# Norm squares of q in batch 1 get slots of hS, and the turning of x of batch 3 is cut in two

## The chip, the core and the metric

The kernel runs on one core of one Trainium2 chip. The metric is the device time of one execution in microseconds (us); the kernel before has a median of 606.14 us over three runs (606.14, 606.62 and 604.99). Five instruction streams run beside each other and meet only at semaphores: TensorE (PE; its weight loads are PEld), VectorE (DVE), ScalarE (ACT), GpSimd (POOL) and SyncE (SP). SP does no arithmetic here: it issues DMAs. ACT issues some DMAs too, and does so in the same stream as its arithmetic. Each stream is executed in the order in which the program wrote it.

## What is computed

Eight batches of x, each 1024 tokens by 256 channels, all float32. Cut to what matters:

```python
xn  = layernorm(x)                                   # no weights
q, k, v = split(xn @ qkv_w + qkv_b)                  # 16 heads of 16 channels
q, k = l2norm(q), l2norm(k)                          # per token and head
kv  = einsum('bhnd,bhne->bhde', k, v)                # linear attention, 16x16 per head
att = einsum('bhnd,bhde->bhne', q, kv) @ proj_w + proj_b
ffn = relu(xn @ W1 + b1) @ W2 + b2                   # 256 -> 1024 -> 256
out = x + att + ffn
```

## The kernel before

**Products by sums.** Nearly all matrix products are done with fewer block products than the plain way: the blocks of both operands are added and subtracted first, and the results are added up afterwards. Those of q and k, of xn^T kn and of the output are 2x2 schemes with seven products (`project_by_sums`, `mix_g_by_sums`, `second`); the hidden layer of batches 1 to 7 is a scheme with 26 products, the list `PRODUCTS`, played out by the list `STEPS` (`hidden`). PE has less to do for it, and DVE, ACT and above all POOL have the sums: POOL makes the forms of x (`FORMS`, L307: s1A, X1 to X10 and so on), those of the hidden layer, and those of xn and kn.

**Stages.** For each batch b the order on PE is: `hidden(b)` (W1 and relu), `project_by_sums(b + 1)` (q and k of the next batch), and `second(b)` (W2 and the projection of the attention, L1112), in the middle of which `mix_g_by_sums(b + 1)` makes g = xn^T kn of the next batch. v is never made: kv comes from g and the weights (`mix_kv`, L755), and `mix_m` (L774) folds it with proj_w into a matrix M that stands beside W2.

**Order by hand.** There is no scheduler: `tc.manual_schedule()` keeps the order of the source on each engine. What is not a matrix product is handed to `second` and `hidden` as callbacks that are played at fixed points. For `second` they are `early`, `mid`, `behind`, `late` and `later` (L1420 to L1460), and where they stand is what this change is about. In `second(b)` the order is: product a, copy u1, product c, `early()`, add u2, product a again, y, `mid()`, turn_back, `behind()`, products f and d, add u3, join(1,0), then six of the seven products of g (`next(of_g)`, L1283), `more_sums_of_x(b + 1, 0)` (X3 to X6 on POOL), `late()`, product e, join(1,1), the seventh product of g, `more_sums_of_x(b + 1, 1)` (X7 to X10 on POOL), `later()`, store of half the output, product e again, join(0,1). A join adds on DVE, transposes 32x32 blocks on DVE (`turn_back`) and adds to the output tile xq on POOL (L1147).

**The norm of q.** `norms_of_q(b)` (L608) squares q of a batch in four pieces of 128x512 on ACT (`squares_of`, L504), sums each piece by head on DVE (L505), inverts the 128x128 sums (`invert`: maximum on DVE L465, root on ACT L466, reciprocal on DVE L467) and scales q on POOL in two halves (`scale`, L624). The squares go to two small buffers that alternate, so the third square waits for the sum of the first; for batch 1 these are the tags `u1` and `y`, for the others the two buffers of `yt`. For batch 1 all this is in `later()` of `second(0)`, after X7 to X10; for later batches it is in `early()`. The scaled q is then turned (`turn_of_q`, four DVE transposes L386, each moved by four DMAs L394) during the next `hidden`, between its sums.

**The turning of x.** `turn_x(b)` does a quarter of the transposition of xn: one DVE transpose of 128x512 (L386) into the tile `turn`, then four DMAs of 64 KB (L394) that carry the squares to xnT. `turn_next()` (L1414) does four of them for batch b + 2 and then `shift` (ACT, L656), which adds one to half of xn. In `second(0)` it stands in `late()` with half of the DMAs on ACT, in `second(1)` in `behind()`, from `second(2)` on in `early()`; there all DMAs are SP's. In `second(1)` it turns batch 3, whose normalization stands just ahead (`mid()`: statistics L344 to L359 and eight ACT applications L368).

**What follows on the queues.** `late()` ends with `load(b + 3)`: two SP DMAs of 512 KB of x (L149). In `second(1)` this is x of batch 4, and `later()` takes its statistics on DVE (`stats_of(4)`: L344, L347, L356, L359) ahead of join(0,1) and of the sums of `hidden(2)` (L1004). SP's next issues are the output store (L1110), the weights of the hidden layer that are loaded anew for each batch (w_sb<-w1f, L898), the second store and the moves of the turned q.

**Slots.** `hS[b]` holds sums of the hidden layer and of q: three kinds by five slots of 128x512. In batch 0 the third kind is free after `first_hidden`; slots 0 to 3 of it hold s1, s4, t1 and t2 of the sums of xn and kn of batch 1 (`g_sums`, L700), and slot 4 (`FH`) held a sum of x. Slots 0, 2 and 3 (s1, t1 and t2) are read last by the first six products of g; s4 in slot 1 is read by the seventh.

Of the kernel before, what the change touches and what calls it, by code (L numbers as in the profile page):

```python
# [9 lines left out]
F32 = mybir.dt.float32  # L10
# [51 lines left out]
def kernel(  # L62
# [35 lines left out]
    P = 128  # L98
    B, N, C = x.shape
    H, D = 16, 16  # L100
    assert H * D == C
    INTER = w1.shape[1]
    NT = N // P
# [6 lines left out]
    R = P // S  # L110
# [7 lines left out]
    one = ctx.enter_context(tc.tile_pool(name="one", bufs=1))  # L118
    work = ctx.enter_context(tc.tile_pool(name="work", bufs=2))
    small = ctx.enter_context(tc.tile_pool(name="small", bufs=2))  # L120
# [19 lines left out]
    xs, xqs, xns, xnTs, xSs, hTs, qks, qTs, mixes, Ms, hSs = ({} for _ in range(11))  # L140
# [105 lines left out]
    HM, FH, HC = INTER // 2, FC // 2, C // 2  # L246
# [46 lines left out]
    def forms_of(b):  # L293

        f = {f"b{k + 1}{u + 1}": xnTs[b][:, k, u, :, :] for k in range(KC) for u in range(NP)}
        f |= {v: xS[:, i] for i, v in enumerate(("s1A", "s2A", "s4A", "s1B", "s2B", "s4B"))}
        f |= {v: as_tokens(half_of_w1t(1, i)) for i, v in enumerate(("dA", "s3B"))}
        f |= {"X1": f["b21"], "X2": f["b14"]}
        return f

    def more_forms_of(b):

        return {
            f"X{3 + i}": qks[b][:, 1, i, :].rearrange("p (c w) -> p c w", w=2) for i in range(8)
        }
# [10 lines left out]
    def make_forms(f, names):  # L316
        for v in names:
            p, op, q = FORMS[v]
            nc.gpsimd.tensor_tensor(f[v], f[p], f[q], ALU.add if op == "+" else ALU.subtract)
# [7 lines left out]
    def more_sums_of_x(b, part):  # L327

        names = [f"X{i}" for i in range(3 + 4 * part, 7 + 4 * part)]
        make_forms(forms_of(b) | more_forms_of(b), names)  # L330
# [45 lines left out]
    class Turn:  # L376
# [21 lines left out]
        def step(self, queues=(nc.sync,)):  # L398
            self.square()
            self.move(queues)  # L400
# [62 lines left out]
    def invert(ss):  # L463

        nc.vector.tensor_scalar_max(ss, ss, L2_EPS * L2_EPS)  # L465
        nc.scalar.activation(ss, ss, AF.Sqrt)  # L466
        nc.vector.reciprocal(ss, ss)  # L467
# [29 lines left out]
    def part_of_qk(b, u, m):  # L497

        return qks[b][:, m, 2 * u : 2 * u + 2, :]

    def squares_of(b, u, m, ss, tag="yt"):
        pool = work if tag == "yt" else one
        sq = pool.tile([P, 2, C], F32, tag=tag, name=f"sq_{b}_{u}_{m}")
        nc.scalar.activation(sq, part_of_qk(b, u, m), AF.Square)  # L504
        return lambda: nc.vector.tensor_reduce(  # L505
            ss[:, 2 * u : 2 * u + 2, :],
            sq.rearrange("p w (g d) -> p w g d", d=D), AX.X, ALU.add,
        )
# [85 lines left out]
    def bias_of_q(b, bias=None):  # L594
        if bias is None:
            bias = bias_in_bank(b)
        for u in (3, 0):
            q1 = part_of_qk(b, u, 0)
            nc.vector.tensor_tensor(
                q1, q1, bias.unsqueeze(1).to_broadcast([P, 2, C]), ALU.add  # L600
            )

    def bias_in_bank(b):
        bias = bank([P, C], f"dbias_{b}")
        nc.scalar.copy(bias, dbias)
        return bias

    def norms_of_q(b):  # L608
        ss = small.tile([P, NT, H], F32, tag="ssq", name=f"ssq_{b}", bufs=1)
        late = []  # L610
        for u in range(NP):
            late.append(squares_of(b, u, 0, ss, ("u1", "y")[u % 2] if b == 1 else "yt"))
            if len(late) == 2:
                late.pop(0)()
        late.pop(0)()
        invert(ss)
        for h in range(2):
            norms_of[b, h, 0] = ss[:, ts(h, HT), :]
            scale(nc.gpsimd, b, h, 0)

    def scale(eng, b, h, s):

        part = qks[b][:, s, ts(h, HT), :].rearrange("p t (g d) -> p t g d", d=D)
        eng.tensor_tensor(  # L624
            part, part,
            norms_of[b, h, s].unsqueeze(3).to_broadcast([P, HT, H, D]), ALU.mult,
        )
# [8 lines left out]
    def turn_q(b):  # L636
        turn_of_q(b).step()
# [15 lines left out]
    def shift(b):  # L653

        part = xns[b][:, :, 0:P]
        nc.scalar.activation(part, part, AF.Identity, bias=ones)  # L656
# [443 lines left out]
    def product(dst, lhs, rhs, start, stop):  # L1100

        for n, (l, r) in enumerate(zip(lhs, rhs)):
            nc.tensor.matmul(  # L1103
                dst, l, r, start=start and n == 0, stop=stop and n == len(lhs) - 1,
                skip_group_check=True,
            )
# [5 lines left out]
    def second(b, early=None, mid=None, behind=None, late=None, later=None):  # L1112
# [16 lines left out]
        def tmp(name):  # L1129
            pool = work if name in ("u2", "yt") else one  # L1130
            return pool.tile([P, HP, P, 2], F32, tag=name, name=f"{name}_o_{b}")
# [5 lines left out]
        def turn_back(n, m, y):  # L1137

            yt = tmp("yt").rearrange("p a b c -> p (a b c)").rearrange(
                "p (u w r c) -> p u w r c", w=2, r=R, c=S  # L1140
            )
            nc.vector.transpose(  # L1142
                yt.rearrange("p u w r c -> p u r w c"),
                y.rearrange("p u (s r) w -> p u r w s", r=R),
            )
            xh = xq[:, n, :, :, ts(m, S)].rearrange("p r t c -> p t r c")
            nc.gpsimd.tensor_tensor(xh, xh, yt.rearrange("p u w r c -> p (u w) r c"), ALU.add)  # L1147

        def join(n, m, bank_, u):
            y = tmp("y")  # L1150
            nc.vector.scalar_tensor_tensor(y, bank_, ob[:, 2, m : m + 1], u, ALU.add, ALU.add)  # L1151
            turn_back(n, m, y)
# [107 lines left out]
        def po(s):  # L1260
            return bank([P, HP, P, 2], f"po{s}_{b}")
# [3 lines left out]
        u1 = tmp("u1")  # L1265
# [5 lines left out]
        y = tmp("y")  # L1271
# [4 lines left out]
        f = po("f")  # L1276
# [10 lines left out]
        product(e, t1, s1, True, False)  # L1287
        join(1, 1, e, u3)
        next(of_g)
        more_sums_of_x(b + 1, 1)  # L1290
        later()
        store(b, 1)
        product(e, b22, s4, False, True)
        join(0, 1, e, u2)


    warm = bank([P, HT, P], "warm")
# [23 lines left out]
    i, mv, rstd = stats.pop((0, 0))  # L1321
# [58 lines left out]
    for b in range(B):  # L1380
        if b == 0:
            first_hidden()
            nc.sync.dma_start(out=w1_sb[:, 0, HM:INTER], in_=w1[0:P, HM:INTER])
        else:
            hidden(b)
        if b == B - 1:
            for _ in second(b):
                pass
            break

        def load_first_w1():
            load_w1(0, 4)
            load_w1(4, 1)

        if b == 0:

            def last_turn():
                turn_q(0)
                sums_of_q(0, "1")
                for i in range(FH):  # L1400
                    sums_of_h(0, i, "2")
                sums_of_q(0, "2")

            of_w1 = forms_of_w1()
            project_by_sums(1, [lambda: turn_q(0), last_turn])
            next(of_w1)
        else:
            load_first_w1()
            load_squares(b)
            if b > 1 and b + 2 < B:  # L1410
                norm_apply(b + 2, range(NT))
            project_by_sums(b + 1)

        def turn_next():  # L1414
            if b + 2 < B:
                for _ in range(R):
                    turn_x(b + 2, (nc.sync, nc.scalar) if b == 0 else (nc.sync,))
                shift(b + 2)

        def early():  # L1420
            g_sums(b + 1, 1)
            g_sums(b + 1, 2)
            for i in (1, 2, 0, 3):
                sums_of_h(b, i, "3")
            sums_of_q(b, "3")
            if b == 0:
                next(of_w1)
                stats_of(2)
                return
            bias_of_q(b + 1)  # L1430
            norms_of_q(b + 1)
            if b > 1:
                turn_next()

        def mid():
            if b == 0:
                norm_apply(2, range(NT))
                next(of_w1)
                load_first_w1()
            elif b == 1:  # L1440
                stats_of(3)
                norm_apply(3, range(NT))

        def behind():
            if b == 1:
                turn_next()

        def late():
            if b == 0:
                bias = bias_in_bank(1)  # L1450
                turn_next()
                bias_of_q(1, bias)
            if b + 3 < B:
                load(b + 3)

        def later():
            if b == 0:
                norms_of_q(1)
            else:
                stats_of(b + 3)  # L1460

        second(b, early, mid, behind, late, later)


# [29 lines left out]
```

## Time and profile before

| what | us |
|---|---|
| median of three runs | 606.14 (604.99 to 606.62) |
| the profiled execution, its own time | 604.75 |
| its span, first to last instruction | 603.0 |
| PE busy | 596.5 |
| POOL busy | 481.0 |
| DVE busy | 435.4 |
| ACT busy | 247.4 |
| granted TensorE clock | 1.000 throughout |

The profile is one execution on the chip: its start and end outside the span make 1.75 us. A line of a timeline gives the start and the length in us, the engine, the source line, the operation, the tile that is written and those that are read, the shape, and how many instructions were merged (x4); in brackets at its end stands how long the engine was idle before it and what released it. "SPq" and "ACTq" are DMA issues. PE instructions are pipelined, so that the length of a group overlaps with the next one's; the distance of starts tells the pace: 0.86 us for a product of the hidden layer or of q and k, 0.89 us for one of g, 4.29 us for one of `second`. The stages that are spoken of lie at: `second(0)` from 67 to 104 us, `hidden(1)` from 104 to 130, `second(1)` from 142 to 179, `hidden(2)` from 179 to 204.

### The profile page before, as it was taken

Reading aid. Unit: us, or ns where it says so; the run is one execution under the profiler, and the core shown is the slowest. Engines: PE = TensorE matmul, PEld = TensorE weight load, DVE = VectorE, ACT = ScalarE, POOL = GpSimd, SP = SyncE. Lnnn points to the kernel's source line nnn. Section 1 sums busy time; section 2 is a strip of 40 time slices with the busy share of each in tenths; the row PEclk is TensorE's granted clock in tenths of the full one; section 3 lists DMA queues with packets and bytes.
Section 4 is the critical chain, followed back from the end, with each engine's and each line's share of the span. In section 5 each row is a group of like instructions: output and inputs, shape, how many; then the busy total and the mean of one; then the engine's idle time right before and its main releaser. Section 6 shows DMA issues by size and latency. Waiting matters only on the chain.

```text
span 603.0 us, 7997 instructions
## 1 busy us (share of the span) xinstructions
PE 596.5 (99%) x2385; PEld 413.2 (69%) x2385; DVE 435.4 (72%) x803; ACT 247.4 (41%) x525; POOL 481.0 (80%) x453
## 2 busy tenths in 40 slices
PE   9999999999999999999999999999999999999997
PEld 5466656786568865688566894678846787468746
DVE  7987976878758785577856878388873669537773
ACT  4654332473405851158311673126730373203810
POOL 2859999988976889769897698976989679983470
PEclk9999999999999999999999999999999999999999
DMA  8545367784056733377134780356702667006704
GB/s 289 87 101 140 82 211 206 183 210 55 10 158 170 194 48 70 108 202 179 19 71 139 197 172 6 99 137 178 158 22 49 144 144 148 2 0 164 185 11 95
DMA packets 164810, 73.02 MB, mean 121 GB/s; under 512 B 147488, under 2 KB 152736, under 8 KB 163872
## 3 DMA queue, kind: packets, MB, share of 16 engines
q1 hardware_dynamic: 154432, 67.31, 46.6%
q10 hardware_dynamic: 10336, 5.21, 3.1%
q8 instruction: 19, 0.31, 0.2%
q14 instruction: 23, 0.19, 0.1%
HBM read 44.44 MB, written 11.80 MB: 93 GB/s over the span
## 4 chain that ended last, share of the span: by engine, by line
PE 86%; DVE 6%; POOL 3%; DMA 2%; ACT 1%; issue 1%; ACTq 0%; DVEq 0%; POOLq 0%
PE ph L985 23%; PE poe L1103 9%; PE poa L1103 9%; PE pod L1103 5%; PE poc L1103 5%; PE pof L1103 4%; PE pqe L530 3%; PE pqa L530 3%; PE pqd L530 3%; PE gpd L728 2%; PE gpe L728 2%; PE gpa L728 2%; PE pqc L530 2%; POOL qk L624 2%; PE tok L1213 2%; PE pq L428 1%
## 5 line engine op out<-in xcount | busy, mean ns | idle before, releaser
L1012 ACT ACTIVATE hT<-hT,b_sb 128x256 f32<-128x256 f32 x224 | 95.7, 497 | 56.1 <-DVE hT L1004 56.1
L1004 DVE TENSOR_TENSOR hT<-ph,hT 128x512 f32<-128x512 f32 x84 | 56.0, 687 | 25.1 <-ACT hT L999 21.6
L1004 DVE TENSOR_TENSOR hT<-hT,ph 128x512 f32<-128x512 f32 x77 | 51.8, 679 | 11.1 <-PE ph L985 7.0
L1103 PE MATMUL poa<-hT,w_sb 128*128 128x512 f32 x120 | 56.2, 593 | 0.0
L504 ACT ACTIVATE sq<-qk 128x512 f32<-128x512 f32 x56 | 34.2, 627 | 49.9 <-DVE qk L536 39.8
L1147 POOL TENSOR_TENSOR xq<-xq,yt_o 128x512 f32<-128x512 f32 x29 | 36.5, 1272 | 22.1 <-DVE yt_o L1142 22.1
L985 PE MATMUL ph<-xnT,w_sb 128*128 128x256 f32 x224 | 52.9, 379 | 0.0
L985 PE MATMUL ph<-qk,w_sb 128*128 128x256 f32 x196 | 48.1, 379 | 0.3 <-DMA w_sb<-w1f 0.3
L239 POOL TENSOR_TENSOR hS<-hT 128x512 f32<-128x512 f32 x30 | 38.3, 1276 | 11.5 <-DVE hT L1004 11.5
L985 PEld LDWEIGHTS ph<-xnT,w_sb 128*128 128x128 f32 x224 | 41.9, 190 | 5.5
L985 PEld LDWEIGHTS ph<-qk,w_sb 128*128 128x128 f32 x196 | 37.2, 190 | 5.7 <-POOL Mt L234 0.7
L999 ACT COPY hT<-ph 128x512 f32<-128x512 f32 x49 | 28.1, 574 | 30.4 <-PE ph L985 30.3
L240 POOL TENSOR_TENSOR hS<-hS,hT 128x512 f32<-128x512 f32 x30 | 38.3, 1277 | 2.4
L1103 PEld LDWEIGHTS poa<-hT,w_sb 128*128 128x128 f32 x120 | 22.7, 190 | 25.4 <-issue 22.7
L242 POOL TENSOR_TENSOR hT<-hT 128x512 f32<-128x512 f32 x30 | 38.5, 1310 | 0.0
L1142 DVE STREAM_TRANSPOSE yt_o<-y_o 128x512 f32<-128x512 f32 x29 | 32.2, 1112 | 8.3 <-ACT y_o L1272 6.1
L244 POOL TENSOR_TENSOR hS<-hT,hS 128x512 f32<-128x512 f32 x30 | 37.7, 1290 | 0.0
L985 PE MATMUL ph<-xS,w_sb 128*128 128x256 f32 x140 | 35.1, 381 | 0.2
L624 POOL TENSOR_TENSOR qk<-qk,ssk 128x1024 f32<-128x1024 f32 x14 | 26.8, 1936 | 9.3 <-DVE ssk L467 9.3
L1151 DVE SCALAR_TENSOR_TENSOR y_o<-poe,ob,u_o 128x512 f32<-128x512 f32 x14 | 10.4, 741 | 31.1 <-PE poe L1103 31.1
L1103 PE MATMUL poe<-hS,w_sb 128*128 128x512 f32 x64 | 30.4, 600 | 0.3
L1103 PE MATMUL poc<-hS,w2t 128*128 128x512 f32 x64 | 29.9, 592 | 0.0
(249 smaller groups left out, 1422.4 us busy)
## 6 DMA issues: line engine op xcount, KB each, us to landing
w_sb<-w1f SPq DMA_DIRECT2D x49, 256.0 KB, 3.5
qT<-turn_q SPq DMA_DIRECT2D x128, 64.0 KB, 3.0
x<-in_L_attn_x_dram SPq DMA_DIRECT2D x15, 512.0 KB, 4.6
xq<-in_L_attn_x_dram SPq DMA_DIRECT2D x60, 128.0 KB, 5.0
out_dram<-xq SPq DMA_DIRECT2D x58, 128.0 KB, 2.9
w_sb<-w1f SPq DMA_DIRECT2D x7, 1024.0 KB, 4.9
xnT<-turn_x SPq DMA_DIRECT2D x104, 64.0 KB, 2.1
w1t<-w1f SPq DMA_DIRECT2D x14, 256.0 KB, 5.3
```

What stands on the lines that cost most here:

```text
L239: eng.tensor_tensor(s1, a21, a22, ALU.add)
L240: eng.tensor_tensor(s2, s1, a11, ALU.subtract)
L242: eng.tensor_tensor(a21, a11, a21, ALU.subtract)
L244: eng.tensor_tensor(s4, a12, s2, ALU.subtract)
L530: nc.tensor.matmul(dst[:, w, :], f[pairs[g][2][i]][:, :, w], pairs[g][3][i], start=start and w == 0, stop=stop, skip_group_check=True,)
L624: eng.tensor_tensor(part, part, norms_of[b, h, s].unsqueeze(3).to_broadcast([P, HT, H, D]), ALU.mult,)
L728: nc.tensor.matmul(dst, l[:, t, :], r[:, t, :], start=start and t == 0, stop=stop and t == HT - 1, skip_group_check=True,)
L985: nc.tensor.matmul(banks[chain][:, t], w[:, t, :], f[v], start=start and t == 0, stop=n == last[chain], skip_group_check=True,)
L1004: nc.vector.tensor_tensor(block(v), operand(p), operand(q), ALU.add if op == "+" else ALU.subtract)
L1012: nc.scalar.activation(part, part, AF.Relu, bias=b1_sb[:, fc : fc + 1])
L1103: nc.tensor.matmul(dst, l, r, start=start and n == 0, stop=stop and n == len(lhs) - 1, skip_group_check=True,)
L1147: nc.gpsimd.tensor_tensor(xh, xh, yt.rearrange("p u w r c -> p (u w) r c"), ALU.add)
```

## The change

It has two parts.

1. **q of batch 1.** Its four squares go to slots 0, 2, 3 and 4 of the third kind of hS of batch 0, one slot each, instead of alternating between two buffers. The squares stand in `late()` of `second(0)` and their sums, the inversion and the scaling in `later()`, through a generator. For b = 0 alone `more_sums_of_x(1, 1)`, the forms X7 to X10, moves from ahead of `later()` to the end of `second`, behind join(0,1).
2. **x of batch 3.** `turn_next` in `behind()` of `second(1)` does two of the four quarters and no shift; the other two and the shift move to `late()`, behind six of the seven products of g and ahead of `load(4)`.

On PE the order of instructions is the same in both kernels. On ACT the four squares stay behind the DMA issues and the shift, and the shift of batch 3 moves behind the two copies of g. On POOL the two scalings of q of batch 1 and the last xq addition stand ahead of the four instructions of X7 to X10. On DVE two of the four transposes of x of batch 3 move behind four additions of g. On SP the order of DMAs is the same.

```diff
-    def squares_of(b, u, m, ss, tag="yt"):
-        pool = work if tag == "yt" else one
-        sq = pool.tile([P, 2, C], F32, tag=tag, name=f"sq_{b}_{u}_{m}")
+    def squares_of(b, u, m, ss, sq=None):
+        if sq is None:
+            sq = work.tile([P, 2, C], F32, tag="yt", name=f"sq_{b}_{u}_{m}")
         nc.scalar.activation(sq, part_of_qk(b, u, m), AF.Square)
...
+    def norms_of_second_q():
+
+        ss = small.tile([P, NT, H], F32, tag="ssq", name="ssq_1", bufs=1)
+        late = [
+            squares_of(
+                1, u, 0, ss,
+                hSs[0][:, 2, i].rearrange("p u c w -> p (u c w)").rearrange("p (w c) -> p w c", w=2),
+            )
+            for u, i in enumerate((0, 2, 3, FH))
+        ]
+        yield
+        for step in late:
+            step()
+        invert_and_scale_q(1, ss)
+        yield
...
         next(of_g)
-        more_sums_of_x(b + 1, 1)
+        if b > 0:
+            more_sums_of_x(b + 1, 1)
         later()
         store(b, 1)
         product(e, b22, s4, False, True)
         join(0, 1, e, u2)
+        if b == 0:
+            more_sums_of_x(b + 1, 1)
...
-        def turn_next():
+        of_q = []
+
+        def turn_next(n=R, shifted=True):
             if b + 2 < B:
-                for _ in range(R):
+                for _ in range(n):
                     turn_x(b + 2, (nc.sync, nc.scalar) if b == 0 else (nc.sync,))
-                shift(b + 2)
+                if shifted:
+                    shift(b + 2)
...
         def behind():
             if b == 1:
-                turn_next()
+                turn_next(2, False)

         def late():
             if b == 0:
                 bias = bias_in_bank(1)
                 turn_next()
                 bias_of_q(1, bias)
+                of_q.append(norms_of_second_q())
+                next(of_q[0])
+            elif b == 1:
+                turn_next(2)
             if b + 3 < B:
                 load(b + 3)

         def later():
             if b == 0:
-                norms_of_q(1)
+                next(of_q[0])
             else:
                 stats_of(b + 3)
```

`invert_and_scale_q` is the last part of `norms_of_q`, unchanged and given a name.

More of the change, by code (lines that the diff above doesn't have):

```diff
@@ L611, in norms_of_q @@
         for u in range(NP):
-            late.append(squares_of(b, u, 0, ss, ("u1", "y")[u % 2] if b == 1 else "yt"))
+            late.append(squares_of(b, u, 0, ss))
             if len(late) == 2:
@@ L615, in norms_of_q, with invert_and_scale_q @@
         late.pop(0)()
+        invert_and_scale_q(b, ss)
+    def norms_of_second_q():
[12 more added lines that the diff above has]
+        yield
+    def invert_and_scale_q(b, ss):
         invert(ss)
```

## The prediction

> **What bounds the kernel.** I read the page's first part, then PE's waits over the whole span, then the chain of work by time, then the timelines of all engines from 90 to 205 us. First the page:
>
> ```profile
> span 603.0 us, 7997 instructions
> PE 596.5 (99%) x2385; PEld 413.2 (69%) x2385; DVE 435.4 (72%) x803; ACT 247.4 (41%) x525; POOL 481.0 (80%) x453
> ```
>
> and the list of what PE waited for (total us, times, longest):
>
> ```profile
> PE warm L1298 <- DVE ones L216: 1.1, 1, 1.1
> PE ph L985 <- DVE hT L1004: 0.7, 2, 0.4
> PE gpd L728 <- DVE u_g L734: 0.6, 1, 0.6
> PE ph L985 <- DMA w_sb<-w1f: 0.3, 1, 0.3
> ```
>
> TensorE is the bound. Its waits come to 2.7 us in all, and 1.6 of them lie where the change is made; no other edit of cover can win anything. The restart after a wait costs more than the wait, so I price stages by starts. `hidden(3)` runs on PE from 252.93 to 277.14: 24.21 us, no wait. `hidden(2)` takes 179.20 to 204.27: 25.07, so 0.86 is lost. `hidden(1)` takes 103.77 to 129.70: 25.93, so 1.72 is lost. In `second(1)`, from the fifth product of g (166.81) to the next product (169.44) it is 2.63 us; in `second(2)` the same steps take 241.39 to 243.17, 1.78; so 0.85 is lost. The change can touch 3.4 us, or 0.57%, and no more.
>
> The waits on PE's timeline:
>
> ```profile
> 112.98 1.10 PE L985 MATMUL ph<-xnT,w1t 128*128 128x256 f32 x4 [0.38 <-DVE hT L1004]
> ...
> 119.25 1.97 PE L985 MATMUL ph<-qk,w_sb 128*128 128x256 f32 x8 [0.30 <-DMA w_sb<-w1f]
> ...
> 168.47 1.13 PE L728 MATMUL gpd<-gt,x 128*128 128x128 f32 x8 [0.60 <-DVE u_g L734]
> ...
> 188.29 1.10 PE L985 MATMUL ph<-xnT,w1t 128*128 128x256 f32 x4 [0.27 <-DVE hT L1004]
> ```
>
> Four stalls are to be seen: two in `hidden(1)`, one in g of batch 2, one in `hidden(2)`.
>
> **Part 1, q of batch 1.** What leads to the scaling, from the timelines of ACT, DVE and POOL:
>
> ```profile
> 101.05 1.15 ACT L656 ACTIVATE x<-x,ones 128x1024 f32<-128x1024 f32 x1 [7.19 <-DMA xnT<-turn_x]
> 102.10 1.14 ACT L504 ACTIVATE sq<-qk 128x512 f32<-128x512 f32 x2
> 103.47 1.22 ACT L504 ACTIVATE sq<-qk 128x512 f32<-128x512 f32 x2 [0.23 <-DVE ssq L505]
> ...
> 102.75 2.67 DVE L505 TENSOR_REDUCE ssq<-sq 128x32 f32<-128x512 f32 x4 [2.11 <-ACT sq L504]
> ...
> 107.08 3.83 POOL L624 TENSOR_TENSOR qk<-qk,ssq 128x1024 f32<-128x1024 f32 x2 [0.81 <-DVE ssq L467]
> ```
>
> POOL waited 0.81 us for the reciprocal, so X7 to X10, done by 106.28, are not what holds the scaling. What holds it are the squares, and these start when ACT has issued its DMAs and done the shift (102.1); the new order leaves both ahead of them. All that goes is the third square's wait of 0.23. DVE's sums are nearly back to back already: starts at 102.75, 103.35 and 104.14, then 0.60 more. With four free slots they go at 0.60 throughout, and the fourth ends 3 x 0.60 + 0.69 behind 102.75, at 105.24 instead of 105.43. The scaling comes **0.19 us** earlier.
>
> Two things follow it. DVE's turn_q at 110.95 waits for POOL, and PE's wait at 112.98 is for an addition behind it: 0.19 off. The last xq addition on POOL, the store and two weight loads behind it on SP (112.18, 114.89) move by 0.19 too, and the wait at 119.25 is for those weights. The two stalls lie one behind the other, so the end of the stage moves by 0.19, not by twice that.
>
> What it costs: X7 to X10 (2.91 us on POOL, 103.37 to 106.28) now come after the xq addition, at about 112.0 to 114.9. X7 is PE's product 19, at about 123.6: covered by 8 us. POOL's next work (g_sums, s3B, s1A, M's sums, s2A and so on) comes 2.9 late and meets POOL's own waits: 1.43 us at 123.03, 0.57 at 126.63, 1.55 at 147.36. Its first forms of batch 2 that PE reads, s1B and s2B, would be done at about 125, and PE asks for them at 130.56. So I cost it at nothing; if this cover were gone, 2.9 less those waits.
>
> Two additions of hT by hT (114.89, taking 1.08, and 116.52, taking 0.64) run beside POOL, and two at 190.22 while POOL waits take 1.28 together. So POOL's work costs the first about 0.44 today. Now POOL's 1.28 us instructions of g_sums stand there. If one addition waits for such a whole instruction, 0.85 more than now, products 13 and 14 (117.82, 119.25) go late, and past the cover of 0.3 some 0.5 is left. If neither waits, 0.44 is won on DVE, but the weights still end the wait. I take -0.19 for part 1; ends -0.3 and +0.5. The nearest row, turn_q to scaling, is the reason.
>
> [...]
>
> **Part 2, x of batch 3.** DVE and SP in `second(1)` and `hidden(2)`:
>
> ```profile
> 162.68 2.49 DVE L386 STREAM_TRANSPOSE turn_x<-x 128x512 f32<-128x512 f32 x4 [3.07 <-ACT x L368]
> ...
> 169.64 0.29 DVE L734 TENSOR_TENSOR gT<-gpd,u_g 128x128 f32<-128x128 f32 x1 [0.99 <-PE gpd L728]
> 173.93 0.75 DVE L1151 SCALAR_TENSOR_TENSOR y_o<-poe,ob,u_o 128x512 f32<-128x512 f32 x1 [4.00 <-PE poe L1103]
> ...
> 177.68 1.41 DVE L344 BATCH_NORM_STATS2 st<-x 128x6 f32<-128x256 f32 x4 [1.61 <-DMA x<-in_L_attn_x_dram]
> ...
> 163.42 10.50 SPq L394 DMA_DIRECT2D xnT<-turn_x  x16
> 174.09 0.96 SPq L149 DMA_DIRECT2D x<-in_L_attn_x_dram  x2
> ```
>
> The gain: four transposes hold DVE from 162.68 to 165.10, 0.605 each. Two fewer bring what follows 1.21 earlier. The addition of u_g at 168.03 comes at 166.97, when PE's fourth product of g is out (166.81 and 0.16 for its tail), and ends by 167.3; PE is ready for the sixth at 167.70. The stall goes: **0.85 us**. The other transposes fall into DVE's idle 4.00 us ahead of 173.93, the shift into ACT's idle 13 us: both free.
>
> The loss is on SP. Its 16 DMAs take 10.50 us, 0.656 each, and x of batch 4 is issued right behind them. Now the ninth waits for the third transpose: the gT addition at 169.64 - 0.85 = 168.79, the transpose 0.21 later (as in `second(0)`, 94.21 to 94.42), the DMA 0.74 after that (162.68 to 163.42): 169.74. Eight more take 5.25, to 174.99; the load follows 0.17 later (173.92 to 174.09) at 175.16. That is **1.07 us late**, 0.88 with the 0.19 of part 1.
>
> This load is on the path. DVE's statistics wait for it, and from 177.68 DVE hardly stops: statistics, join, turn_q, the sums of hT, until the addition at 189.61 that PE's product 10 (190.35) waits for; its pauses (0.18 for the second half of the load, 0.37 and 0.23 for ACT) move with it. So product 10 goes from 190.35 to 191.23, however early PE came from g. The 0.85 won is waited for in `hidden(2)`, with 0.88 on top. Behind product 10 PE runs without a wait, and the 0.88 stays to the end. Bounds of the load's landing: it may land as before, if the bytes of the turn ahead of it and not its issue set the time (0 for part 2), or take a microsecond longer (below).
>
> Sum: 604.75 + 0.88 = 605.6 for the profiled execution, whose time stands 1.39 below the median: **607.0 us**.
>
> **Rivals.** (a) The forecast: the load's issue sets `hidden(2)`; 606.5 to 607.7; chance 0.56, of which a tenth has the +0.5 of part 1. (b) The load lands where it did: the stall moves from g into `hidden(2)` and only part 1 is left or nothing: 606.0; for it, other loads land in 2.6 to 6.5 us, so issue is not all; against it, this one's halves landed 3.6 and 4.6 after their issue with the same queue ahead; 0.20. (c) Slower: the output store, which waits for the join after g, comes 1 us earlier, at about 176, and the load's bytes are now still in flight. In `second(0)`, with a store 2.1 us behind the load, the halves took 4.6 and 5.5, 1.0 longer: 606.14 + 0.88 + 1.0 = 608.0. It is past 0.3% once the first half lands more than 0.94 later after its issue than before; 0.14. Against it, there the moves of two queues were ahead of the load. (d) The 0.85 and 0.19 both stay, because DVE's row of work has slack that I don't see: 605.1; 0.10.
>
> [...]
>
> **Numbers.** A measurement of this kernel can tell about 0.3%, 1.8 us, from no change: 604.3 to 608.0. (a), (b) and (d) lie inside, (c) on the edge. Faster 0.04, within 0.82, slower 0.14. The range reaches from (d) to (c) with part 1's upper end: 605.0 to 608.5.
>
> **What would show it.** Right: the wait of gpd is gone; the load of x is issued near 175; DVE's wait for it ends near 178.6; PE's two stalls in `hidden(2)` cost some 2.8 us (0.86 + 0.88 + the 1.04 by which PE arrives earlier) instead of 0.86; POOL idles over 3 us ahead of the scaling, which starts near 106.9. Wrong: the load is issued by 174.1, or `hidden(2)` gets shorter, or the scaling starts a microsecond earlier.

## The result, and the profile after

The changed kernel takes 606.53 us (median of 11 runs, 605.95 to 607.98), the kernel before 604.99 (11 runs, 604.38 to 606.62). The ratio is 1.0023, with a 95% interval of 1.0012 to 1.0034: 1.4 us slower (0.7 to 2.1), which is within the 0.3% taken as no change. The forecast was 0.9 slower. The profiled execution took 606.75. Two runs of the experiments below stand far off the others of their kernel and are left out of medians and ratios: one of e1 with 624.67 us, the one that was profiled, and one of e2 with 3611.23.

The head of the page:

```profile
span 605.0 us, 7996 instructions
PE 596.4 (99%) x2385; PEld 412.3 (68%) x2385; DVE 435.5 (72%) x803; ACT 247.0 (41%) x525; POOL 480.8 (79%) x453
```

PE's work is the same to 0.1 us, and the span is 2.0 longer: all of it is waiting. The four longest rows of what PE waited for (total us, times, longest):

```profile
PE ph L1004 <- DVE hT L1023: 2.2, 2, 2.0
PE warm L1320 <- DVE ones L216: 1.1, 1, 1.1
PE ph L1004 <- DMA w_sb<-w1f: 0.6, 1, 0.6
PE gp L682 <- POOL qk L643: 0.6, 1, 0.6
```

The wait of g for u_g is gone, and the wait of the hidden layer for hT has grown from 0.7 to 2.2. The last of these rows lies between 31 and 39 us, far ahead of `hidden(1)` and in code that is the same in both kernels. `hidden(1)` starts at 104.39 instead of 103.77; over the profiles of all the kernels below this start lies anywhere from 103.48 to 105.43, whichever part of the change they have. So these 0.62 us are not put down to the change, and below the stages are counted from the first product of `hidden(1)`. Products of the hidden layer are counted from 0, as in the prediction. PE's timeline:

```profile
119.37 1.89 PE L1004 MATMUL ph<-qk,w_sb 128*128 128x256 f32 x8
...
127.06 1.99 PE L1004 MATMUL ph<-xnT,w_sb 128*128 128x256 f32 x8 [0.61 <-DMA w_sb<-w1f]
...
168.62 1.06 PE L747 MATMUL gpd<-gt,x 128*128 128x128 f32 x8
169.52 1.88 PE L1122 MATMUL poe<-hS,w2t 128*128 128x512 f32 x4
...
190.25 1.10 PE L1004 MATMUL ph<-xnT,w1t 128*128 128x256 f32 x4 [1.96 <-DVE hT L1023]
```

Three things are to be seen. In `hidden(1)` PE no longer waits for weights at product 14 (119.37, and 119.25 before), but now for those of product 22, at 127.06. The sixth product of g, at 168.62, has no bracket any more: that stall is gone. And the stall in `hidden(2)` has grown from 0.27 to 1.96. From its line to the end of `hidden(2)` it is 15.98 us in both kernels, so nothing behind it has changed.

The weights that product 22 reads leave on SP behind a store and eight moves of the turned q, in the changed kernel and then in the one before:

```profile
112.67 2.62 SPq L1129 DMA_DIRECT2D out_dram<-xq  x4
...
117.15 2.58 SPq L394 DMA_DIRECT2D qT<-turn_q  x4
...
120.47 2.56 SPq L394 DMA_DIRECT2D qT<-turn_q  x4
123.13 1.02 SPq L917 DMA_DIRECT2D w_sb<-w1f  x2
```

```profile
122.62 1.02 SPq L898 DMA_DIRECT2D w_sb<-w1f  x2
```

ACT, DVE and POOL at q of batch 1:

```profile
102.80 2.17 ACT L504 ACTIVATE hS<-qk 128x512 f32<-128x512 f32 x4
...
103.44 2.46 DVE L505 TENSOR_REDUCE ssq<-hS 128x32 f32<-128x512 f32 x4 [2.17 <-ACT hS L504]
105.94 0.23 DVE L465 TENSOR_SCALAR ssq<-ssq 128x128 f32<-128x128 f32 x1
...
107.57 3.83 POOL L643 TENSOR_TENSOR qk<-qk,ssq 128x1024 f32<-128x1024 f32 x2 [3.53 <-DVE ssq L467]
115.47 1.73 POOL L712 TENSOR_TENSOR x<-x 128x512 f32<-128x512 f32 x1
```

The four squares run without a pause, their sums take 2.46 instead of 2.67, and the scaling starts 3.18 us behind the first product of `hidden(1)` instead of 3.31. POOL sits idle for 3.53 us ahead of it, as it has given X7 to X10 away. DVE and SP around the turning of x of batch 3:

```profile
163.79 1.31 DVE L386 STREAM_TRANSPOSE turn_x<-x 128x512 f32<-128x512 f32 x2 [3.07 <-ACT x L368]
...
167.93 0.29 DVE L753 TENSOR_TENSOR u_g<-gpd,u_g 128x128 f32<-128x128 f32 x1
...
169.92 1.30 DVE L386 STREAM_TRANSPOSE turn_x<-x 128x512 f32<-128x512 f32 x2
174.01 0.75 DVE L1170 SCALAR_TENSOR_TENSOR y_o<-poe,ob,u_o 128x512 f32<-128x512 f32 x1 [2.79 <-PE poe L1122]
...
179.65 1.41 DVE L344 BATCH_NORM_STATS2 st<-x 128x6 f32<-128x256 f32 x4 [3.50 <-DMA x<-in_L_attn_x_dram]
...
164.58 11.27 SPq L394 DMA_DIRECT2D xnT<-turn_x  x16
176.01 0.96 SPq L149 DMA_DIRECT2D x<-in_L_attn_x_dram  x2
177.35 3.33 SPq L1129 DMA_DIRECT2D out_dram<-xq  x4
```

DVE finishes u_g at 168.22, before PE wants it at 168.62. The second half of the turn starts at 169.92, and its eight DMAs end SP's row of sixteen at 175.85 (164.58 and 11.27). The load of x of batch 4 follows at once, at 176.01, and DVE's statistics wait 3.50 us for it instead of 1.61.

### The profile page after: what moved, and what is told of

It reads as the page before. It is cut to its first block, busy times and chain, and to the rows that moved or that the text cites. A ratio compares the mean times of both kernels' runs of the same rounds, so it can differ in the third digit from the quotient of the medians.

```text
span 605.0 us, 7996 instructions
## 1 busy us (share of the span) xinstructions
PE 596.4 (99%) x2385; PEld 412.3 (68%) x2385; DVE 435.5 (72%) x803; ACT 247.0 (41%) x525; POOL 480.8 (79%) x453
## 4 chain that ended last, share of the span: by engine, by line
PE 89%; DVE 5%; DMA 2%; ACT 1%; POOL 1%; SPq 1%; issue 1%; ACTq 0%; DVEq 0%
PE ph L1004 22%; PE poa L1122 11%; PE poe L1122 9%; PE poc L1122 6%; PE pod L1122 6%; PE pof L1122 5%; PE pqe L530 4%; PE pqa L530 4%; PE pqd L530 3%; PE gpd L747 2%; PE gpa L747 2%; PE pqc L530 2%; PE gpe L747 2%; PE tok L1232 2%; PE pq L428 1%; PE gp L682 1%
## 5 line engine op out<-in xcount | busy, mean ns | idle before, releaser
L504 ACT ACTIVATE sq<-qk 128x512 f32<-128x512 f32 x52 | 31.8, 627 | 49.8 <-DVE qk L536 39.9
L239 POOL TENSOR_TENSOR hS<-hT 128x512 f32<-128x512 f32 x30 | 38.3, 1277 | 10.9 <-DVE hT L1023 10.9
```

What stands on the lines that cost most here:

```text
L239: eng.tensor_tensor(s1, a21, a22, ALU.add)
```

## Experiments

The theory: the loss is the issue of `load(4)`, which stands on SP behind moves that now start later; the stall of g is truly gone, but what it wins is waited for in `hidden(2)`. The rivals: that the late transposes and the late shift hold DVE's and ACT's own rows back; that traffic in flight delays the load; that part 1 makes the loss. The table has the kernels with a profile that compares stage by stage, us between first products of PE; "load" is the issue of `load(4)` counted from the end of `hidden(1)`. Ratios are against the kernel before, with 95% intervals, from 11 runs of a kernel but for e2 (8), e12 (6), e8 (5) and e11 (4); each row of stages is one profile.

| kernel | hidden(1) | q, k, second(1) | hidden(2) | sum | load | ratio |
|---|---|---|---|---|---|---|
| before | 25.93 | 49.50 | 25.07 | 100.50 | 44.39 | 1 |
| after | 26.22 | 48.67 | 26.95 | 101.84 | 45.40 | 1.0023 [1.0012, 1.0034] |
| e2 part 2 alone | 25.62 | 48.66 | 28.20 | 102.48 | 45.39 | 1.0028 [1.0012, 1.0044] |
| e13 part 1 alone | 25.84 | 49.92 | 24.88 | 100.64 | 44.92 | one run |
| e3 load first | 25.94 | 48.66 | 24.20 | 98.80 | 39.49 | 0.9977 [0.9968, 0.9985] |
| e4 load on ACT | 25.98 | 48.66 | 24.21 | 98.85 | 40.80 | 0.9980 [0.9971, 0.9988] |
| e10 before, load on ACT | 25.47 | 49.55 | 24.20 | 99.22 | 40.03 | 0.9986 [0.9977, 0.9995] |
| e11 three quarters late | 25.46 | 48.66 | 29.49 | 103.61 | 48.03 | 1.0069 [1.0052, 1.0086] |
| e5 slots alone | 25.97 | 49.48 | 25.04 | 100.49 | 44.37 | one run |
| e6 X7 to X10 alone | 25.52 | 49.19 | 24.91 | 99.62 | 44.20 | one run |
| e9 e3 without part 1 | 26.08 | 48.67 | 24.20 | 98.95 | 39.21 | 0.9979 [0.9970, 0.9988] |
| e8 e3, weights first | 25.25 | 48.66 | 24.20 | 98.11 | 39.21 | 0.9962 [0.9950, 0.9975] |
| e12 e8 without part 1 | 25.59 | 48.66 | 24.21 | 98.46 | 39.21 | 0.9966 [0.9953, 0.9978] |

Diffs are against the changed kernel, but for e10.

### The parts alone

**e1_part1** (and **e13_part1_look**, the same kernel once more, for its stages): the turn of batch 3 is put back.

```diff
         def behind():
             if b == 1:
-                turn_next(2, False)
+                turn_next()
...
-            elif b == 1:
-                turn_next(2)
```

> Part 1 of the change alone (q of batch 1: squares in slots of hS, X7 to X10 behind the scaling); the turning of x of batch 3 as before. Theory A (SP's queue decides both parts): in hidden(1) PE no longer waits for the weights of products 14 and 15, arrives earlier at product 22 and waits there for the next weights, whose issue stands behind the store and eight moves of q on SP; hidden(1) takes 25.7 to 26.2 us against 25.93 before, and the time changes by -0.2 to +0.3 us. In second(1) PE's wait for u_g (0.60) is still there, hidden(2) keeps 25.07 within 0.1. Theory B (POOL's late X7 to X10 and g_sums hold DVE's additions up): PE's waits for hT at products 9 and 13 grow, hidden(1) takes 26.4 or more and the time is up by 0.5 or more.

> Part 1 alone once more, for its stages. If part 1 moves only where PE waits in hidden(1): turn_q at 6.95 to 7.05 us behind product 0, hidden(1) between 25.4 and 26.2 (as in kernels with and without part 1), second(1) 49.5 with the wait for u_g, hidden(2) 25.0 to 25.1; from product 0 of hidden(1) to the end of hidden(2) 99.9 to 100.8, against 100.50 before. If part 1 costs time by itself: over 100.9.

Measured: 605.07 against 604.82, ratio 1.0002 [0.9992, 1.0011]; the one run of e13 gave 605.12 against 605.01. Part 1 by itself can't be told from nothing. The stages of e13 say how: turn_q starts 6.98 behind the first product of `hidden(1)` instead of 7.18, so the scaling is indeed 0.2 earlier, and the wait at product 14 is gone. But PE then stands at product 22:

```profile
126.24 1.99 PE L1004 MATMUL ph<-xnT,w_sb 128*128 128x256 f32 x8 [0.29 <-DMA w_sb<-w1f]
```

**e2_part2**: part 1 is put back.

```diff
-                of_q.append(norms_of_second_q())
-                next(of_q[0])
...
             if b == 0:
-                next(of_q[0])
+                norms_of_q(1)
...
-        if b > 0:
-            more_sums_of_x(b + 1, 1)
+        more_sums_of_x(b + 1, 1)
...
-        if b == 0:
-            more_sums_of_x(b + 1, 1)
```

(The squares go back to the buffers `u1` and `y` as well.)

> Part 2 alone (half of the turning of x of batch 3 behind six products of g); q of batch 1 as before. Theory A (the load of x of batch 4 stands behind the turn's moves on SP, is issued 1.07 us later, and DVE's statistics and all its work up to product 10 of hidden(2) follow it): the load is issued about 1.0 to 1.1 later against product 0 of hidden(1), PE's wait for u_g is gone, PE's wait for hT in hidden(2) grows to about 2.0, and the time goes up by 0.9 to 1.2 us. Theory B (the load lands when it did): the time stays within 0.3 us. Theory C (the 0.85 is kept): down by 0.8.

Measured: 606.52 against 604.82, 1.0028 [1.0012, 1.0044]. Part 2 alone makes the loss: its load is issued 1.00 later than before and `second(1)` is 0.84 shorter, both as in the changed kernel. `hidden(2)` is 1.25 longer than there, though the stall is the same (1.95): that is the TensorE clock, of which the last section tells.

### The load

**e3_load_first**: `load(4)` goes ahead of the second half of the turn; that half, the transposes and the shift stay late.

```diff
             elif b == 1:
+                load(b + 3)
                 turn_next(2)
-            if b + 3 < B:
+            if b != 1 and b + 3 < B:
                 load(b + 3)
```

> The changed kernel with one line moved: in second(1) the load of x of batch 4 is put ahead of the second half of the turning, so on SP it stands behind eight moves of x of batch 3, not sixteen; it has only to wait for the last reader of x of batch 2 (g and a sum on POOL). DVE, ACT and POOL keep the order of the changed kernel. Theory A (the load's issue decides): the load goes out near 170 instead of 176, DVE's statistics don't wait, PE waits neither in g nor at products 9 and 10 of hidden(2), which falls from about 27.1 to 24.2 us; the time is 2.5 to 3 us below the changed kernel, and 1.2 to 1.8 below the kernel before. Theory B (not the load but the two DVE transposes and the shift on ACT, now late, hold hidden(2) up): no gain against the changed kernel.

Measured: 603.45, ratio 0.9977 [0.9968, 0.9985]: faster than both kernels. SP and DVE:

```profile
164.28 5.21 SPq L394 DMA_DIRECT2D xnT<-turn_x  x8
169.65 0.96 SPq L149 DMA_DIRECT2D x<-in_L_attn_x_dram  x2
170.71 5.23 SPq L394 DMA_DIRECT2D xnT<-turn_x  x8
...
175.60 2.70 DVE L344 BATCH_NORM_STATS2 st<-x 128x6 f32<-128x256 f32 x8
```

The row of sixteen is cut in two and the load stands in the gap. The statistics at 175.60 have no bracket: DVE comes to them from its own work and waits for nothing. `hidden(2)` takes 24.20, just what `hidden(3)` takes, which never had a stall. The eight moves behind the load end at 175.94, as late as in the changed kernel (175.85), and DVE's and ACT's late work is all still there; so neither holds anything back. That rival falls.

**e4_load_on_act**: the load stays where it is in the program, but ACT's queue issues it.

```diff
             if b + 3 < B:
-                load(b + 3)
+                load(b + 3, queue=nc.scalar if b == 1 else nc.sync)
```

(`load` takes the queue as an argument for it.)

> The changed kernel with the load of x of batch 4 issued by ACT, behind the shift of x of batch 3, which ACT starts at about 171.3; SP keeps all its other DMAs in their order. Theory A (only the time of this load's issue decides): it goes out near 172.5 instead of 176, DVE's statistics start about 3 earlier, near 176.5, so hidden(2) loses little or nothing: 24.2 to 24.6 us, and the time is 2.3 to 2.9 below the changed kernel. Theory B (the transfers share the DMA engines, so that the load lands late however early it is issued, beside the eight moves of the turn): it lands little earlier, a gain under 1 us.

Measured: 603.57, 0.9980 [0.9971, 0.9988], `hidden(2)` 24.21. This differs from the changed kernel in the queue alone, and it takes away the whole loss. The bytes of the turn are still moved around the load: SP's sixteen moves even took 14.71 us to issue beside it instead of 11.27.

```profile
163.54 14.71 SPq L394 DMA_DIRECT2D xnT<-turn_x  x16
...
170.32 0.85 ACTq L149 DMA_DIRECT2D x<-in_L_attn_x_dram  x2
```

What traffic can do to the load is small: behind the sixteen moves its halves landed 3.6 and 4.6 us after issue in the kernel before, and 3.6 and 4.7 in the changed one; amid them, in e4, DVE comes to the first half 4.64 us after issue (at 174.96) and waits for nothing, and its eight statistics take 2.81 against 2.70 in e3. So the first half lands about a microsecond later after its issue at most; the place in SP's queue is worth 4.6 here (45.40 less 40.80), and it is this that makes the loss.

**e10_before_load_act**: the same edit in the kernel before, all else of the change undone.

> The kernel before, neither part of the change, with the load of x of batch 4 issued by ACT instead of SP. Theory A (the load's issue alone sets hidden(2); part 2's 0.85 in g is a separate gain): PE's wait for u_g in second(1) stays, second(1) takes 49.5 us, hidden(2) falls from 25.07 to about 24.2, and the time is 0.7 to 1.0 us below the kernel before, about 0.85 above the kernel with part 2 and the load first. Theory B (the load is only a symptom, hidden(2) is held by DVE's other work): hidden(2) stays at 25.

Measured: 604.00 against 604.82, 0.9986 [0.9977, 0.9995]. `hidden(2)` falls from 25.07 to 24.20, and the wait for u_g stays (0.65). So with the early load the stall of g, 49.55 against 48.66 in e4, is a loss of its own: 0.89 us that part 2 takes away, once nothing behind it takes it back. By time this is not shown in full: 0.85 was expected between e10 and the kernels with part 2 and an early load, and e4 is 0.43 faster, with intervals that overlap. In the profiles `hidden(1)` is 0.51 longer in e4 than in e10, which leaves 0.37 of the 0.89.

**e11_three_late**: three of the four quarters late instead of two.

```diff
-                turn_next(2, False)
+                turn_next(1, False)
...
-                turn_next(2)
+                turn_next(3)
```

> The changed kernel with three quarters of the turning of x of batch 3 behind the products of g instead of two. Dose test of the load's issue: it stands behind twelve late moves instead of eight, 4 x 0.656 = 2.6 us later than in the changed kernel; second(1) stays at 48.7. Theory A: hidden(2) grows by 2.6 to about 29.5, and the time is 2.4 to 2.8 us above the changed kernel, 3.7 to 4.2 above the kernel before (ratio 1.006 to 1.007). If the landing were set by the engines' bytes: less than half of that.

Measured: 608.79 against 604.82, 1.0069 [1.0052, 1.0086]. Four more moves late put the load 2.63 later than in the changed kernel (four issues of 0.656: 2.62), and `hidden(2)` is 2.54 longer. Here a microsecond of issue is a microsecond of the stage, to within 0.1.

### Inside part 1

**e5_slots_only** keeps the new slots for the squares and leaves X7 to X10 ahead of `later()`; **e6_xmove_only** does the reverse. Both turn x of batch 3 as before. For e5:

```diff
-        if b > 0:
-            more_sums_of_x(b + 1, 1)
+        more_sums_of_x(b + 1, 1)
...
-        if b == 0:
-            more_sums_of_x(b + 1, 1)
```

and, for e6,

```diff
-                of_q.append(norms_of_second_q())
-                next(of_q[0])
...
             if b == 0:
-                next(of_q[0])
+                norms_of_q(1)
```

> Of part 1 only the squares' slots in hS (and their place in late); X7 to X10 stay ahead of the scaling, the turning of x of batch 3 as before. If the squares set the scaling: it starts as early against product 0 as with part 1 whole (turn_q at 6.9 to 7.1 us behind product 0, against 7.18 before), and POOL waits about 0.6 ahead of it; PE's wait for weights at product 22 shows as with part 1 whole, 0.2 to 0.6. If X7 to X10 set it: turn_q at 7.2. POOL's sums of xn (L712) take 1.27 to 1.28 us, as before.

> Of part 1 only the move of X7 to X10 behind the last join; the squares as before. If the squares set the scaling: turn_q at 7.15 to 7.25 us behind product 0, as before, POOL waits over 3 us ahead of the scaling, and hidden(1) takes 25.6 to 26.0. If X7 to X10 had held the scaling: turn_q at 7.05 or earlier. POOL's two sums of xn beside the two additions of hT by hT take 1.6 to 1.75 instead of 1.28, as in the changed kernel.

Measured, one run each: 605.51 and 604.12, beside about 604.8 for the kernel before; a single run can't rank these. What they tell is where the scaling's 0.2 us come from. In neither does turn_q start earlier: 7.22 and 7.17 behind the first product, against 7.18 before and 7.05 after. In e6 the third square still waits for a buffer. In e5 the sums are quick (2.47), but then, on DVE and on POOL:

```profile
106.04 0.43 DVE L465 TENSOR_SCALAR ssq<-ssq 128x128 f32<-128x128 f32 x1
...
105.65 1.42 POOL L319 TENSOR_TENSOR qk<-qk,xnT 128x256 f32<-128x256 f32 x2
```

The small maximum takes 0.43 beside X9, the first of these two on POOL, where it takes 0.23 in the changed kernel with POOL idle. It is not X9 alone but when the maximum meets it: in the kernel before and in e5 the maximum starts 0.58 and 0.39 behind X9 and takes 0.23 and 0.43, so that it ends 0.81 and 0.82 behind X9's start; why it ends there is not shown. Here sums that end sooner only bring it further into X9; that eats what the slots won. In these profiles both halves of part 1 are needed for its 0.2.

### The weights of product 22, and the best version

**e9_p2_first** is e3 without part 1. **e8_all** is e3 with the weights for products 22 and 23 issued ahead of four moves of q, and **e12_no_part1** is e8 without part 1.

```diff
-        steps[11] += squares_at(11) + weights(10) + move()
+        steps[11] += squares_at(11) + weights(10) + (move() if b != 1 else [])
         steps[12] += forms("dA")
-        steps[13] += squares_at(13) + forms("s4A", "X1") + weights(11)
+        steps[13] += squares_at(13) + forms("s4A", "X1") + weights(11) + (move() if b == 1 else [])
```

> The kernel with the load of x of batch 4 first, without part 1 (q of batch 1 as in the kernel before). Theory A (part 1 is worth nothing as it stands: its 0.2 at products 9 and 14 comes back as a wait at product 22): hidden(1) takes 25.6 to 25.95 us, the time is within 0.3 us of the kernel with the load first and part 1, about 1.4 below the kernel before. Theory B (part 1 costs time, by POOL's later sums): 0.3 to 0.5 below the kernel with the load first. Theory C (part 1 is a gain): 0.2 or more above it.

> The kernel with the load of x of batch 4 first, and one more line moved: in hidden(1) the weights of products 22 and 23 are issued ahead of four moves of q instead of behind them (for batch 1 alone). Theory A (part 1 wins time ahead of product 22 and loses it there, because these weights are issued behind the store and eight moves of q): the weights go out as soon as product 13 is done, some 3 us earlier, PE's wait for them (0.43 to 0.61 us) goes, hidden(1) falls from 25.9 to 26.2 to about 25.3 us, and the time is 0.4 to 0.8 us below that of the kernel with the load first alone, so 1.7 to 2.3 below the kernel before. Theory B (the wait is for the DMA engines' bytes, not for the issue): the weights land as late as before, no gain, or the moves of q that now come later hold the projection up in second(1).

> The fastest kernel so far (part 1, part 2, load first, the weights of products 22 and 23 ahead of four moves of q) without part 1. Theory A (part 1's 0.2 is real once product 22 doesn't wait): hidden(1) takes 25.4 to 25.6 us against 25.25, the time is 0.1 to 0.4 us above it. Theory B (part 1 is worth nothing even then): the same within 0.1. Theory C (part 1 costs): below it.

Measured: e9 603.55, ratio 0.9979 [0.9970, 0.9988]; e8 603.07, 0.9962 [0.9950, 0.9975]; e12 602.96, 0.9966 [0.9953, 0.9978]. SP in e8:

```profile
119.06 1.01 SPq L917 DMA_DIRECT2D w_sb<-w1f  x2
120.17 2.57 SPq L394 DMA_DIRECT2D qT<-turn_q  x4
```

Two loads of weights now go out together, ahead of the four moves, and the wait at product 22 is gone. `hidden(1)` takes 25.25, the shortest of all, 0.69 less than in e3. e8 is 2.3 us faster than the kernel before (1.5 to 3.0) and beats the changed kernel; whether it needs part 1 can't be told: e8 and e12 have the same ratio within their intervals, e9 and e3 too.

## Why the prediction was right, point by point

- **The stall of g goes, 0.85.** Right. `second(1)` with q and k fell by 0.83, and to 48.66 or 48.67 in every kernel with half the turn late. e10 against e4 shows it to be a gain of its own.
- **The load is issued 1.07 late.** Right in mechanism and size: 1.01 (45.40 against 44.39). The stall's product in `hidden(2)`, counted from the end of `hidden(1)`, moved from 58.59 to 59.64, 1.05. The two stalls of `hidden(2)` were to cost 2.8 and cost 2.74 (26.95 less the 24.21 of `hidden(3)`). e3, e4 and e11 show that this issue alone sets it.
- **The transposes and the shift in the idle time, free.** Right: they are late in e3 and e4 too, and `hidden(2)` takes 24.20 there.
- **Part 1, 0.19 off the stage.** Half wrong. The scaling came 0.13 earlier in the changed kernel, 0.2 in e13, and the addition that PE waits for with it. The step that failed is that "the end of the stage moves by 0.19, not by twice that": I followed two stalls and not the next deadline behind them. PE came to product 14 0.50 earlier and lost it at product 22, whose weights are issued behind a store and eight moves of q. In the changed kernel's profile this made 0.29 more instead of 0.19 less. The weights were issued 0.11 earlier there (18.74 behind the stage's first product instead of 18.85) but landed 3.9 us after issue instead of 3.5, and in e2, with the same order, 3.1: the 0.29 of this one profile is no more than what the landing varies by. Over all profiles, `hidden(1)` with part 1 and the old order of weights is 25.46 to 26.22 long, without it 25.47 to 26.08: when these weights land matters more than part 1. By time part 1 alone is worth between -0.5 and +0.7 us.
- **X7 to X10 on POOL, free.** Right. POOL's waits of 1.43 and 0.57 behind them are gone, and the sum at L239 that waited at 126.63 starts at 127.76 without a wait. The additions of hT by hT took 0.68 and 1.13 instead of 1.08 and 0.64: POOL's part of their cost went from the first to the second, and the end at +0.5 did not come. That end was an estimate of mine for an addition that waits for a whole 1.28 us instruction of POOL, and no run shows one: the longest of these additions took 1.13, 0.49 more than the 0.64 of one while POOL waits.
- **The rivals.** (b), the load lands as before, fell: its landing moved with its issue. (c), it lands a microsecond later behind its issue, fell too: the store is now issued 1.34 us after it, and its halves landed 3.6 and 4.7 us after issue, against 3.6 and 4.6. (d), hidden slack, fell with the stall of 1.96.
- **The sum.** Between the first product of `hidden(1)` and the end of `hidden(2)` the profiles differ by 1.34: 0.29 and 1.05, where the forecast had -0.19 and 1.07. By time it is 1.4, or 1.35 with the eight runs of the changed kernel whose clock did not dip (last section). The mis-sized term is part 1's, by 0.5. The time itself is 606.5 against 607.0: the forecast started from the median of three runs, and 11 runs of the kernel before have one that is 1.15 lower; this and the 0.5 of part 1 partly cancel, so that the time came this near is partly luck.

What stays open: why `second(1)` with q and k is 0.42 longer in e13 than before, in code that is the same in both, which shows how much single profiles differ; why the kernel before waits for weights at product 14 in its profile and in e5, and not in e2, e6 or e10, with the same issue times behind the start of the stage; and whether part 1 is worth nothing or the 0.34 by which `hidden(1)` differs between e8 and e12.

## What to carry to other kernels

When a step is put off, ask what its DMAs stand in front of on their queue: sixteen moves of 64 KB cost their queue 10.50 us of issue in the kernel before and 11.27 in the changed one, and a load behind them is late by as much as they are, wherever the compute itself finds room. A gain early in a chain counts only up to the next deadline that did not move with it; here an earlier load, two lines in the program, turned 1.4 us lost into 1.4 won. When a stall goes, find what PE waits for next, before the sum is made.

## What the runs showed of the hardware

The same stall did not always cost the same. In e2 PE stood idle for 2.12 us ahead of the stalled product, just as in the changed kernel, but there the clock then fell. The stretches from 192 to 193 us in the changed kernel and then in e2 (stretch, length; busy time of PE, PEld, DVE, ACT and POOL; granted clock, DMA share, GB/s):

```profile
192.00:193.00 1.00, 0.91 (x5) 0.64 (x4) 1.00 (x3) 0.75 (x3) 0.08 (x1) 1.00 0.81 254
```

```profile
192.00:193.00 1.00, 1.00 (x4) 0.78 (x3) 1.00 (x2) 0.36 (x1) 0.00 (x0) 0.50 0.81 201
```

The last figure but two is the granted clock, 1.00 against 0.50. In e2 it is 0.50 from 191.5 to 194.9, which is 3.4 us; products take 1.6 to 1.7 us instead of 0.86, and from the stall to the end of `hidden(2)` it is 17.30 us instead of 15.98: 1.3 lost. e11 shows the same dip, 3.4 us from 186.3 to 189.7, behind a stall of 2.51, but ahead of a wait for DVE that hides most of it. Half the clock for 3.4 us of some 606 makes a mean clock of 0.997, and that is what these two profiles have. Such a mean is found in 3 of the 11 runs of the changed kernel (606.68, 607.63 and 607.98, against a median of 606.34 for the others), 3 of 8 in e2 and 4 of 4 in e11; none of the 64 runs of the kernel before beside the experiments, and none of the 55 of e3, e4, e8, e9, e10 and e12, lies below 0.999. Where the dip lay in those without a trace isn't known.

Behind the same 2.12 us of idle time the clock fell in one profiled execution and not in the other; why is not shown. On this kernel, which is bound by PE (busy for 99% of the span), a stall of two microseconds thus carried a risk of about one more, 1.3 in e2.
